# Attention over windows followed by a gated FFN: the third transposition of the probabilities moved into the dense tile, exponentials behind its copy, mixing and norms dealt to other slots

## The chip, the cores and the metric

The kernel runs on one core of a Trainium2 chip. The metric is the device time of one execution in microseconds; lower is better. All data is fp32.

## The reference

The input x is 4 x 2048 x 512. Cut to what matters, with `ln` the layer norm without weights:

```python
def attention(x):                       # x: (4, 2048, 512), 16 heads of 32, windows of 128
    q, k, v = split(x @ w_qkv, 3)
    k_ctx, v_ctx = windows n-1, n, n+1  # three blocks of 128 keys; outside the sequence masked
    attn = softmax((q * 32**-0.5) @ k_ctx.T)
    return attn @ v_ctx

def ffn(x):                             # H=512, F=2048, E=8 experts
    h = relu(x @ gate_w1.T + gate_b1)
    g = mean over the sequence of (h @ gate_w2.T + gate_b2)      # (batch, 8)
    mW1 = W1 + sum_e g[e] * TW1[e];  mb1 = b1 + g @ Tb1
    mW2 = W2 + sum_e g[e] * TW2[e];  mb2 = b2 + g @ Tb2
    return gelu(x @ mW1.T + mb1) @ mW2.T + mb2

x = x + ln(attention(ln(x)))
x = x + ln(ffn(ln(x)))
```

The expert weights are mixed once per batch element, after its gate is known.

## The kernel before

Every instruction's order is written out by hand; the engines work their queues in that order and wait for each other by semaphores. There are two stages: attention, with the gate and part of the mixing, and the FFN, which holds the rest of the mixing.

**Attention** runs over 256 slots, numbered i. A window W of 128 queries takes four slots, g = 0 to 3, of four heads each (i = 4W + g). In the loop of lines 550 to 577 slot i does this:

1. `first[i]`: loads.
2. `scores(i + 1)`: TensorE writes the scores of the next slot's four heads into two PSUM tiles `sc` of two heads each (L404), and VectorE takes the negated row maxima `nm` (L413). The pool `ps_s` has two buffers of such tiles: one slot's worth.
3. `turn(i, 0)` and `turn(i, 1)`: TensorE transposes the probabilities `pr` of key blocks 0 and 1 (L441), ScalarE copies the result to `prT` (L443). The pool `ps_t` has two buffers.
4. `exponentials(i + 1)`: four ScalarE activations read `sc` and `nm`, write `pr` and sum the rows into `den` (L426; each is followed by an accumulator read).
5. `dense[i]`, if there is one: one output tile of 128 x 512 of the projections to q, k or v (`project`, L353) or of the gate (`gate_matmuls`, L163), four matmuls in the program and eight in the trace, into the single buffer `pm`.
6. `turn(i, 2)`, if the window has three key blocks (the first and last window of a sequence have two).
7. The evacuation of the dense tile: q, v and the gate on ScalarE, k on VectorE (L359).
8. `aux[i]`, `values(i)` and the rest of `aux[i]`. `values` multiplies prT with v, key block by key block (L458). `aux` holds the transposition of the previous window's output with its scaling and statistics (g = 0, L223 to L236), that of the second norm (g = 3, L252 to L258), and `place_tile`, which transposes a tile of the next block of x after its norm (L339, L340).
9. `rest[i]`: the residual sum and its statistics (g = 1), the second norm (g = 2), and the first norm of a coming block: `norm_stats` and `norm_tile`, by VectorE with two small GpSimd operations.
10. From slot 84 on, one or two steps of `blend`, the mixer of lines 102 to 159.

A **block K** is four windows (512 rows). Its slots begin at s0 = 4 (4K - 5): in s0 to s0 + 3 its four tiles are placed, in the 12 slots after that its q, k and v are projected. The gate of an earlier block has the dense tiles of slots s0 to s0 + 3.

A **step of mixing** is one `acc + g[e] * expert[e]` over 128 x 1024 (L144), or, after the eighth expert, four smaller VectorE sums over quarters of the tile (L152 to L155). Loads of experts are issued on SyncE three steps ahead into four buffers. All loads and stores go through SyncE's queue.

The **FFN** stage takes 16 blocks, seven products each instead of eight by a Strassen-like scheme, with the remaining steps of mixing between them. It is not touched by the change.

Of the kernel before, what the change touches and what calls it, by code (L numbers as in the profile page):

```python
# [9 lines left out]
F32 = mybir.dt.float32  # L10
# [6 lines left out]
P = 128  # L17
NB, L, D = 4, 2048, 512
# [3 lines left out]
KC = D // P  # L22
TB = 512
# [11 lines left out]
def sandwich(ctx: ExitStack, tc: tile.TileContext, x, w_qkv, gw1, gb1, gw2, gb2, w1, b1, w2, b2, tw1, tb1, tw2, tb2, out):  # L35
# [49 lines left out]
    def stats(src, tag):  # L85

        st = small.tile([P, 6], F32, tag="st", name=f"st_{tag}")
        nc.vector.bn_stats(st, src)
        mv = small.tile([P, 2], F32, tag="mv", name=f"mv_{tag}")
        nc.vector.bn_aggr(mv, st)  # L90
        ve = small.tile([P, 1], F32, tag="ve", name=f"ve_{tag}")
        nc.gpsimd.tensor_scalar(ve, mv[:, 1:2], EPS, None, ALU.add)  # L92
        rs = small.tile([P, 1], F32, tag="rs", name=f"rs_{tag}")
        nc.gpsimd.tensor_tensor(rs, ve, mhalf, ALU.pow)
        return mv, rs

    def normalize(dst, src, sm):
        mv, rs = sm
        nc.vector.tensor_scalar(dst, src, mv[:, 0:1], rs, ALU.subtract, ALU.mult)
# [58 lines left out]
        for f in late:  # L158
            f()

    def gate_matmuls(pm, xT, oc):
        for kc in range(KC):
            nc.tensor.matmul(pm, lhsT=gw1_sb[:, kc, ts(oc, P)], rhs=xT[:, kc, :], start=(kc == 0), stop=(kc == KC - 1))  # L163

    def gate_sum(pm, K, oc, hsum, spare):
        hr = spare(f"hr_{K}_{oc}")
        k = K % NBLK
        nc.scalar.activation(hr, pm, AF.Relu, bias=gb1_sb[:, oc : oc + 1], accum_out=hsum[:, oc, k : k + 1])
# [120 lines left out]
    with ExitStack() as actx:  # L289
        qkvp = actx.enter_context(tc.tile_pool(name="qkvp", bufs=2))  # L290
        work = actx.enter_context(tc.tile_pool(name="work", bufs=2))
# [3 lines left out]
        ps_m = actx.enter_context(tc.tile_pool(name="ps_m", bufs=1, space=PSUM))  # L295

        def load_tile(K, t, tag, bufs):
            b, k = divmod(K, NBLK)
            xt = qkvp.tile([P, D], F32, tag=tag, bufs=bufs, name=f"{tag}_{K}_{t}")
            nc.sync.dma_start(xt, x[b, k * TB + t * P : k * TB + (t + 1) * P])  # L300
            return xt

        x_of, xs_of, xn_of, xnT_of, q_of, k_of, v_of, gT_of = {}, {}, {}, {}, {}, {}, {}, {}
# [21 lines left out]
        def norm_stats(K, t):  # L325
            xs_of[K, t] = stats(x_of[K, t], f"a{K}_{t}")

        def norm_tile(K, t):
            xn = work.tile([P, D], F32, tag="xn", name=f"xn_{K}_{t}")
            normalize(xn, x_of.pop((K, t)), xs_of.pop((K, t)))  # L330
            xn_of[K, t] = xn

        def place_tile(K, t, evac):
            if t == 0:
                xnT_of[K] = qkvp.tile([P, KC, TB], F32, tag="xnT", bufs=2, name=f"xnT_{K}")
            pt = ps_t.tile([P, KC, P], F32, tag="pt", name=f"pt_a{K}_{t}")
            xn = xn_of.pop((K, t))
            for kc in range(KC):
                nc.tensor.transpose(pt[:, kc, :], xn[:, ts(kc, P)], ident)  # L339
            evac(xnT_of[K][:, :, ts(t, P)], pt)  # L340

        def project(K, i, m, pm):

            if m == 0:
                d, name = (q_of, k_of, v_of)[i], "qkv"[i]
                d[K] = qkvp.tile([P, KC, TB], F32, tag=name, name=f"{name}_{K}")
            xnT = xnT_of[K]
            for kc in range(KC):
                if i < 2:
                    l, r = wqkv[i][:, kc, ts(m, P)], xnT[:, kc, :]  # L350
                else:
                    l, r = xnT[:, kc, ts(m, P)], wqkv[2][:, kc, :]
                nc.tensor.matmul(pm, lhsT=l, rhs=r, start=(kc == 0), stop=(kc == KC - 1))  # L353

        def projected(K, i, m, pm):
            if i == 0:
                nc.scalar.mul(q_of[K][:, m, :], pm, QSCALE)
            elif i == 1:
                nc.vector.tensor_copy(k_of[K][:, m, :], pm)  # L359
            else:  # L360
                nc.scalar.copy(v_of[K][:, m, :], pm)  # L361

        def span_of(W_):
            b, w = divmod(W_, NW)
            lo, hi = max(w - 1, 0), min(w + 1, NW - 1)
            return b * NW + lo, hi - lo + 1
# [51 lines left out]
        def exponentials(i):  # L418
            W_, g = divmod(i, KC)
            nk = span_of(W_)[1]  # L420
            st = win[W_]
            scs = st.pop(("sc", g))
            for r in range(4):
                h = g * 4 + r
                pr = work.tile([P, 3 * W], F32, tag="pr", bufs=8, name=f"pr_{i}_{r}")
                nc.scalar.activation(  # L426
                    pr[:, : nk * W],
                    scs[r // 2][:, r % 2, : nk * W],
                    AF.Exp,
                    bias=st["nm"][:, h : h + 1],  # L430
                    accum_out=st["den"][:, h : h + 1],
                )
                st["pr"][h] = pr

        def turn(i, j):

            W_, g = divmod(i, KC)
            st = win[W_]
            pt = ps_t.tile([P, 4, W], F32, tag="pt", name=f"ptp_{i}_{j}")
            for r in range(4):  # L440
                nc.tensor.transpose(pt[:, r, :], st["pr"][g * 4 + r][:, ts(j, W)], ident)  # L441
            prT = work.tile([P, 4, W], F32, tag="prT", bufs=4, name=f"prT_{i}_{j}")
            nc.scalar.copy(prT, pt)  # L443
            st["prT"][g, j] = prT
# [25 lines left out]
        dense = {i: None for i in slots}  # L470
        aux = {i: [] for i in slots}
        rest = {i: [] for i in slots}
        first = {i: [] for i in slots}
        for K in range(1, NBK):
            s0 = 4 * (4 * K - 5)
            if K > 1:
                for t in range(WB):
                    first[s0 + t - 6].append(lambda K=K, t=t: x_of.__setitem__((K, t), load_tile(K, t, "x", 4)))
                    rest[s0 + t - 3].append(lambda K=K, t=t: norm_stats(K, t))
                    rest[s0 + t - 2].append(lambda K=K, t=t: norm_tile(K, t))  # L480
                    aux[s0 + t].append(lambda K=K, t=t: place_tile(K, t, nc.vector.tensor_copy))
            for n, i in enumerate((0, 1, 2)):
                for m in range(KC):
                    dense[s0 + 4 + 4 * n + m] = (
                        lambda pm, K=K, i=i, m=m: project(K, i, m, pm),
                        lambda pm, K=K, i=i, m=m: projected(K, i, m, pm),
                    )

# [6 lines left out]
        def load_gate(K):  # L495
            gT_of[K] = qkvp.tile([P, KC, TB], F32, tag="xnT", bufs=2, name=f"gT_{K}")
            nc.sync.dma_start(gT_of[K], xT_d[K])

        gate_at = {K: 4 * (4 * (K + 3) - 5) for K in range(11)} | {11: 204, 12: 220, 13: 236, 14: 248}
        for K, s0 in gate_at.items():  # L500
            first[s0 - 2].append(lambda K=K: load_gate(K))
            for oc in range(KC):
                dense[s0 + oc] = (
                    lambda pm, K=K, oc=oc: gate_matmuls(pm, gT_of[K], oc),
                    lambda pm, K=K, oc=oc: gate_sum(pm, K, oc, hsum_of[K // NBLK], spare),
                )
            if K % NBLK == NBLK - 1:
                b = K // NBLK
                for j, f in enumerate(gate_end(b, hsum_of[b], spare, spare_bank)):
                    rest[s0 + KC + j].append(f)  # L510
# [19 lines left out]
        for t in range(WB):  # L530
            norm_tile(0, t)
            place_tile(0, t, nc.scalar.copy)
# [17 lines left out]
        for i in range(NS):  # L550
            W_, g = divmod(i, KC)
            nk = span_of(W_)[1]
            for f in first[i]:
                f()
            if i + 1 < NS:
                scores(i + 1)
            turn(i, 0)
            turn(i, 1)
            if i + 1 < NS:
                exponentials(i + 1)  # L560
            if dense[i]:
                pm = ps_m.tile([P, TB], F32, tag="pm", name=f"pm_{i}")
                dense[i][0](pm)
            if nk == 3:
                turn(i, 2)
            if dense[i]:
                dense[i][1](pm)
            for f in aux[i][:1]:
                f()
            values(i)  # L570
            for f in aux[i][1:]:
                f()
            for f in rest[i]:
                f()
            if i >= 84:
                for _ in range(1 if i % 3 == 2 else 2):
                    next(blend)


# [338 lines left out]
```

## Time and profile before

| | us |
|---|---|
| median of 3 runs | 3506.17 |
| lowest and highest | 3504.3, 3508.7 |
| profiled execution, its own time | 3506.56 |
| its span in the profile | 3504.8 |
| TensorE busy in the span | 3381.1 |
| VectorE busy | 2034.2 |
| ScalarE busy | 1476.4 |
| GpSimd busy | 734.2 |

A row of the timeline gives the start in us, the time from the start of the first to the end of the last instruction of a group, the engine, the line, the operation, output and inputs, how many, and in brackets how long the engine had been idle and what ended it. PE is TensorE, PEld its weight load, DVE VectorE, ACT ScalarE, POOL GpSimd, SPq the queue of DMA issues. A row of waits reads: who waited for whom, us in total, times, longest. A row of windows reads: the stretch and its length, the busy time and number of instructions of PE, PEld, DVE, ACT and POOL, the share of TensorE's clock that was granted, the DMA engines' share and GB/s.

### The profile page before, as it was taken

The page shows a single profiled execution, that of the slowest core. Times are in us where ns is not written, and L with a number is a line of the kernel's source. Part 1 is how long each engine was busy: PE and PEld are TensorE (multiplying, and loading weights), DVE is VectorE, ACT ScalarE, POOL GpSimd, SP SyncE. Part 2 cuts the span into 40 slices and gives each one's busy share as a digit, 9 for nine tenths or more (in the row PEclk, how much of TensorE's full clock was granted, in tenths as well). Part 3 has the DMA queues.
Part 4 walks back from the last instruction along what each step waited for, and adds up shares of the span by engine and source line. Part 5 has one row for each costly group of instructions (what it writes and reads, how often), then busy time and mean ns, then how long its engine had stood idle before and what let it go on. Part 6 is the DMA issues. An engine that isn't in the chain of part 4 may idle for free.

```text
span 3504.8 us, 55562 instructions
## 1 busy us (share of the span) xinstructions
PE 3381.1 (96%) x21712; PEld 2427.0 (69%) x21712; DVE 2034.2 (58%) x2868; ACT 1476.4 (42%) x3882; POOL 734.2 (21%) x776
## 2 busy tenths in 40 slices
PE   8999999999999999999988999999999999999998
PEld 4555555555555555555555888888888888888887
DVE  2545455677776777776776367666675774222222
ACT  2666666566565666665665222211112222221121
POOL 0100111122211221221111232223322332122222
PEclk9999999999999999999999999999999999999999
DMA  2111111355564555564567588998889885533332
GB/s 80 40 53 40 40 58 52 130 190 188 196 215 147 188 193 182 187 201 162 177 208 250 198 288 294 349 341 310 294 306 358 297 304 186 183 121 121 120 117 75
DMA packets 315192, 651.76 MB, mean 186 GB/s; under 512 B 22953, under 2 KB 88617, under 8 KB 294450
## 3 DMA queue, kind: packets, MB, share of 16 engines
q1 hardware_dynamic: 314930, 648.22, 53.4%
q8 instruction: 170, 2.79, 0.3%
q14 instruction: 92, 0.75, 0.1%
HBM read 538.03 MB, written 110.10 MB: 185 GB/s over the span
## 4 chain that ended last, share of the span: by engine, by line
PE 80%; DVE 9%; ACT 5%; DMA 3%; issue 2%; SPq 0%; ACTq 0%; DVEq 0%
PE pm L353 15%; PE px L600 11%; PE px L693 9%; PE ptp L441 8%; PE pz L693 6%; PE pz L600 5%; PE sc L404 5%; PE pm L163 5%; PE po L458 4%; DVE acc L144 3%; PE py L693 3%; ACT pr L426 3%; PE py L600 3%; PE py2b L693 3%; DMA exps<-in_tw 2%; ACT prT L443 2%
## 5 line engine op out<-in xcount | busy, mean ns | idle before, releaser
L144 DVE SCALAR_TENSOR_TENSOR acc<-exps,g,acc 128x1024 f32<-128x1024 f32 x512 | 690.5, 1349 | 210.0 <-DMA exps<-in_tw 205.4
L443 ACT COPY prT<-ptp 128x512 f32<-128x512 f32 x736 | 408.5, 589 | 544.8 <-PE ptp L441 544.4
L426 ACT ACTIVATE pr<-sc,nm 128x384 f32<-128x384 f32 (+1 forms) x1024 | 569.0, 576 | 130.5 <-DVE nm L413 130.2
L413 DVE TENSOR_REDUCE nm<-sc 128x2 f32<-128x768 f32 (+1 forms) x512 | 448.0, 916 | 255.7 <-PE sc L404 238.0
L441 PEld LDWEIGHTS ptp<-ident,pr 128*128 128x128 f32 x2944 | 342.3, 145 | 225.2 <-issue 209.0
L353 PE MATMUL pm<-xnT,wqkv 128*128 128x512 f32 x1024 | 465.5, 598 | 3.6 <-DVE k L359 1.6
L441 PE MATMUL ptp<-ident,pr 128*128 128x128 f32 x2944 | 429.5, 284 | 2.3 <-ACT prT L443 2.3
L600 PE MATMUL px<-tT,w 128*128 128x256 f32 x1536 | 359.1, 382 | 9.0 <-DVE cpv L658 9.0
L633 ACT COPY cpa<-px 128x512 f32<-128x512 f32 x64 | 37.2, 581 | 766.4 <-PE px L600 766.4
L600 PEld LDWEIGHTS px<-tT,w 128*128 128x128 f32 x1536 | 293.2, 191 | 51.5 <-DVE cpv L658 11.2
L353 PEld LDWEIGHTS pm<-xnT,wqkv 128*128 128x128 f32 x1024 | 187.0, 193 | 195.5 <-issue 188.1
L458 PE MATMUL po<-prT,v 128*32 128x128 f32 x5888 | 239.7, 281 | 79.8 <-ACT prT L443 79.6
L92 POOL TENSOR_SCALAR ve_b<-mv_b 128x1 f32<-128x1 f32 x64 | 43.6, 682 | 1174.3 <-DVE mv_b L90 1114.8
L404 PE MATMUL sc<-k,q 32*128 32x384 f32 (+2 forms) x2816 | 252.9, 437 | 5.1 <-ACT pr L426 3.8
L458 PEld LDWEIGHTS po<-prT,v 128*32 128x32 f32 x5888 | 138.8, 109 | 159.7 <-ACT prT L443 110.9
L353 PE MATMUL pm<-wqkv,xnT 128*128 128x512 f32 x512 | 230.5, 593 | 0.5 <-ACT v L361 0.5
L693 PE MATMUL px<-w2s,u 128*128 128x256 f32 x1024 | 229.7, 380 | 0.7 <-ACT last L257 0.7
L426 ACT ACTIVATION_READ_ACCUMULATOR pr<-sc,nm 128x1 f32 x1024 | 219.8, 215 | 0.0
L163 PE MATMUL pm<-gT,gw_sb 128*128 128x512 f32 x480 | 218.6, 598 | 0.0
L693 PEld LDWEIGHTS px<-w2s,u 128*128 128x128 f32 x1024 | 195.2, 191 | 27.7 <-ACT last L257 0.9
L670 POOL TENSOR_TENSOR t<-u 128x512 f32<-128x512 f32 x64 | 87.4, 1366 | 461.0 <-ACT u L612 448.9
L404 PEld LDWEIGHTS sc<-k,q 32*128 32x128 f32 x2816 | 122.1, 190 | 61.0 <-issue 39.3
(127 smaller groups left out, 4483.7 us busy)
## 6 DMA issues: line engine op xcount, KB each, us to landing
exps<-in_tw SPq DMA_DIRECT2D x512, 512.0 KB, 5.8
w2s<-m2d SPq DMA_DIRECT2D x112, 1024.0 KB, 5.6
acc<-in_w SPq DMA_DIRECT2D x64, 512.0 KB, 5.9
x<-in_x SPq DMA_DIRECT2D x64, 256.0 KB, 3.9
m1d<-acc SPq DMA_DIRECT2D x64, 256.0 KB, 6.0
m2d<-acc SPq DMA_DIRECT2D x64, 256.0 KB, 6.7
w<-m1d SPq DMA_DIRECT2D x16, 1024.0 KB, 9.4
fxT<-xTd SPq DMA_DIRECT2D x16, 1024.0 KB, 8.3
```

The costliest lines, as they stand in the source:

```text
L144: nc.vector.scalar_tensor_tensor(acc, ets.pop(n), g_all[b][:, e : e + 1], acc, ALU.mult, ALU.add)
L163: nc.tensor.matmul(pm, lhsT=gw1_sb[:, kc, ts(oc, P)], rhs=xT[:, kc, :], start=(kc == 0), stop=(kc == KC - 1))
L353: nc.tensor.matmul(pm, lhsT=l, rhs=r, start=(kc == 0), stop=(kc == KC - 1))
L404: nc.tensor.matmul(scs[r // 2][:, r % 2, col : col + nj * W], lhsT=q[rows, g, ts(W_ % WB, W)], rhs=k_of[kb][rows, g, j0 * W : (j0 + nj) * ...
L413: nc.vector.tensor_reduce(st["nm"][:, h : h + 2], scs[u][:, :, : nk * W], AX.X, ALU.max, negate=True)
L426: nc.scalar.activation(pr[:, : nk * W], scs[r // 2][:, r % 2, : nk * W], AF.Exp, bias=st["nm"][:, h : h + 1], accum_out=st["den"][:, h : h ...
L441: nc.tensor.transpose(pt[:, r, :], st["pr"][g * 4 + r][:, ts(j, W)], ident)
L443: nc.scalar.copy(prT, pt)
L458: nc.tensor.matmul(st["po"][r * E : (r + 1) * E, g, :], lhsT=v_of[kb][:, jj, h * E : (h + 1) * E], rhs=prT[:, r, :], start=(j == 0), stop= ...
L600: nc.tensor.matmul(bank[:, f, :], lhsT=factor[:, f, kc * P : (kc + 1) * P], rhs=right[:, kc, :], start=(start and f == 0 and kc == 0), sto ...
L670: nc.gpsimd.tensor_tensor(t1s[c], b12, S["u"][:, :, :Q], ALU.subtract)
L693: nc.tensor.matmul(bank[:, t, :], lhsT=right(c - c % 2)[:, c % 2, ts(t, P)], rhs=w[:, c, :], start=(start and c == t == 0), stop=True, ski ...
```

## The change

In the slot, the dense tile is split after two of its four matmuls. `turn(i, 2)` is put between the halves, and `exponentials(i + 1)` behind `turn(i, 2)`, so that on ScalarE the copy of the third transposition comes ahead of the exponentials. `project` and `gate_matmuls` get the range of matmuls to do.

The norm of a coming block's tile is written over its x tile, not into a tile of its own. For blocks 3 and up, tile t has its statistics in slot s0 - 14 + 4t and its norm in the slot after it, one tile per window; its load is issued two slots ahead of the statistics, at the end of a slot. For block 2 the statistics and the norm keep their slots, and the load moves by one.

From slot 84 on the four slots of a window take 1, 1, 2 and 3 steps of mixing, every third window 1, 1, 2 and 2, where each slot took 2, 2 and 1 in turn before.

```diff
         def norm_tile(K, t):
-            xn = work.tile([P, D], F32, tag="xn", name=f"xn_{K}_{t}")
-            normalize(xn, x_of.pop((K, t)), xs_of.pop((K, t)))
-            xn_of[K, t] = xn
+            xn = xn_of[K, t] = x_of.pop((K, t))
+            normalize(xn, xn, xs_of.pop((K, t)))
...
                 for t in range(WB):
-                    first[s0 + t - 6].append(lambda K=K, t=t: x_of.__setitem__((K, t), load_tile(K, t, "x", 4)))
-                    rest[s0 + t - 3].append(lambda K=K, t=t: norm_stats(K, t))
-                    rest[s0 + t - 2].append(lambda K=K, t=t: norm_tile(K, t))
+
+                    i = s0 - 14 + 4 * t if K > 2 else s0 + t - 3
+                    rest[i - 2].append(lambda K=K, t=t: x_of.__setitem__((K, t), load_tile(K, t, "x", 4)))
+                    rest[i].append(lambda K=K, t=t: norm_stats(K, t))
+                    rest[i + 1].append(lambda K=K, t=t: norm_tile(K, t))
                     aux[s0 + t].append(lambda K=K, t=t: place_tile(K, t, nc.vector.tensor_copy))
...
             turn(i, 0)
             turn(i, 1)
+            if dense[i]:
+                pm = ps_m.tile([P, TB], F32, tag="pm", name=f"pm_{i}")
+                dense[i][0](pm, range(KC // 2))
+            if nk == 3:
+                turn(i, 2)
             if i + 1 < NS:
                 exponentials(i + 1)
             if dense[i]:
-                pm = ps_m.tile([P, TB], F32, tag="pm", name=f"pm_{i}")
-                dense[i][0](pm)
-            if nk == 3:
-                turn(i, 2)
-            if dense[i]:
+                dense[i][0](pm, range(KC // 2, KC))
                 dense[i][1](pm)
...
             if i >= 84:
-                for _ in range(1 if i % 3 == 2 else 2):
+                for _ in range((1, 1, 2, 2 if W_ % 3 == 2 else 3)[g]):
                     next(blend)
```

More of the change, by code (lines that the diff above doesn't have):

```diff
@@ L159, in mixer, with gate_matmuls @@
             f()
-    def gate_matmuls(pm, xT, oc):
-        for kc in range(KC):
+    def gate_matmuls(pm, xT, oc, kcs=range(KC)):
+        for kc in kcs:
             nc.tensor.matmul(pm, lhsT=gw1_sb[:, kc, ts(oc, P)], rhs=xT[:, kc, :], start=(kc == 0), stop=(kc == KC - 1))
@@ L340, in place_tile, with project @@
             evac(xnT_of[K][:, :, ts(t, P)], pt)
-        def project(K, i, m, pm):
-            if m == 0:
+        def project(K, i, m, pm, kcs=range(KC)):
+            if m == 0 and kcs[0] == 0:
                 d, name = (q_of, k_of, v_of)[i], "qkv"[i]
@@ L347, in project @@
             xnT = xnT_of[K]
-            for kc in range(KC):
+            for kc in kcs:
                 if i < 2:
@@ L484, in sandwich @@
                     dense[s0 + 4 + 4 * n + m] = (
-                        lambda pm, K=K, i=i, m=m: project(K, i, m, pm),
+                        lambda pm, kcs, K=K, i=i, m=m: project(K, i, m, pm, kcs),
                         lambda pm, K=K, i=i, m=m: projected(K, i, m, pm),
@@ L503, in sandwich @@
                 dense[s0 + oc] = (
-                    lambda pm, K=K, oc=oc: gate_matmuls(pm, gT_of[K], oc),
+                    lambda pm, kcs, K=K, oc=oc: gate_matmuls(pm, gT_of[K], oc, kcs),
                     lambda pm, K=K, oc=oc: gate_sum(pm, K, oc, hsum_of[K // NBLK], spare),
```

## The prediction

> **What bounds the kernel now.** I read the page first, for the bound; then the waits, for what TensorE waits for; then the timeline slot by slot, since a share over the span mixes two stages. The attention stage, which alone is changed, runs from the start to about 1905 us.
>
> ```profile
> span 3504.8 us, 55562 instructions
> PE 3381.1 (96%) x21712; PEld 2427.0 (69%) x21712; DVE 2034.2 (58%) x2868; ACT 1476.4 (42%) x3882; POOL 734.2 (21%) x776
> ```
> ```profile
> ACT prT L443 <- PE ptp L441: 544.4, 432, 4.1
> ...
> ACT pr L426 <- DVE nm L413: 130.2, 92, 4.1
> ...
> PE po L458 <- ACT prT L443: 79.6, 108, 3.3
> ```
>
> TensorE is the bound, and its 124 us without work (3504.8 - 3381.1) are mostly one wait: values() on the copy of the transposed probabilities. Why that copy is late shows in a timeline. An undisturbed slot that also transposes an output:
>
> ```profile
> 798.23 0.93 PE L404 MATMUL sc<-k,q 32*128 32x384 f32 x8
> ...
> 799.09 1.09 PE L441 MATMUL ptp<-ident,pr 128*128 128x128 f32 x8
> ...
> 800.01 3.60 PE L353 MATMUL pm<-wqkv,xnT 128*128 128x512 f32 x8
> ...
> 800.79 0.60 ACT L426 ACTIVATE pr<-sc,nm 128x384 f32<-128x384 f32 x1
> ...
> 802.93 0.23 ACT L426 ACTIVATION_READ_ACCUMULATOR pr<-sc,nm 128x1 f32 x1
> ...
> 803.45 0.60 PE L441 MATMUL ptp<-ident,pr 128*128 128x128 f32 x4
> ...
> 804.14 0.59 ACT L443 COPY prT<-ptp 128x512 f32<-128x512 f32 x1 [0.98 <-PE ptp L441]
> ...
> 805.21 0.93 PE L404 MATMUL sc<-k,q 32*128 32x384 f32 x8
> ```
>
> From scores to scores 6.98 us, all of it TensorE's. Without an output transposition the slot takes 6.91: values() then stands 0.16 us before its third block, because the last copy begins only 0.69 us after the third transposition, and TensorE loses as much again in draining. In a slot where VectorE is late it looks like this:
>
> ```profile
> 836.54 2.57 DVE L144 SCALAR_TENSOR_TENSOR acc<-exps,g,acc 128x1024 f32<-128x1024 f32 x2
> ...
> 839.03 1.82 DVE L413 TENSOR_REDUCE nm<-sc 128x2 f32<-128x768 f32 x2
> ...
> 840.02 0.58 ACT L426 ACTIVATE pr<-sc,nm 128x384 f32<-128x384 f32 x1 [3.68 <-DVE nm L413]
> ...
> 842.26 0.60 ACT L443 COPY prT<-ptp 128x512 f32<-128x512 f32 x1
> ...
> 842.91 0.65 PE L458 MATMUL po<-prT,v 128*32 128x128 f32 x8 [2.41 <-ACT prT L443]
> ```
>
> VectorE still mixes two experts while the row maxima are due; the exponentials wait for the maxima, the copy behind them on ScalarE waits too, TensorE waits for the copy. I compared each slot from 84 on (where mixing begins) with undisturbed slots of its kind. Lost by lateness: 29 us in the 28 three-block slots that place a new block (their norms and statistics lie just before and in them), 19 us in the other three-block slots, 6 us in two-block ones: 54 us. The slots around the three gate ends lose 29 us (some of it their own matmuls), those without a dense tile 41 us.
>
> **What is removed.** (1) values() no longer needs a copy that stands behind the exponentials. (2) Statistics and norms of a block, four tiles in five adjoining slots, become one tile per window, in slots 2 and 3. (3) Mixing becomes 1, 1, 2, 3 (every third window 2) instead of 2, 2, 1: 20 steps in 12 slots both ways, so nothing moves to the FFN stage. VectorE's load of a window, from the rows: maxima 4 x 1.82, output scaling and its statistics 1.8 in slot 0, residual and statistics 2.1 in slot 1, second norm 0.53 in slot 2, seven steps of about 1.35: 21 us in 27, or 22.5 with a tile's 0.87 of statistics and 0.53 of norm. It fits; only the order was bad. New worst cases: a k-slot (evacuation 0.69, ready only when the dense tile ends) with three mixing steps lets the next maxima start at about 3.2 us after the first transpositions, against 2.8 wanted below: 0.3 to 0.5 us, in 11 windows; the placing slots 2 and 3 are like it. I leave 10 us of the 54. Gain 44 (bounds 20 and 54).
>
> **A rule of the skill here.** After each of the five 2.41 us waits in placing slots the granted clock is halved, and the next slot is 1.2 to 2.8 us too long, 9 us together (inside the 29):
>
> ```profile
> 833.60:842.60 9.00, 6.89 (x57) 4.34 (x56) 8.69 (x14) 3.66 (x11) 3.73 (x4) 1.00 0.22 61
> 842.70:846.10 3.40, 3.19 (x29) 2.48 (x30) 3.30 (x5) 0.83 (x3) 1.90 (x2) 0.50 0.58 172
> ```
>
> The Trainium skill ("TensorE: Matmul & The Clock Gate", Part 1) says that TensorE falls to half rate after an idle window of about 3.4 us. By it a 2.41 us wait costs only itself, the half-rate stretches have another cause, and the gain is 35 (in the sum below 30 for 39). By the trace, five of five follow such a wait at once and, in slots with a dense tile, none follows a wait up to 1.5 us: they go with it. I take the trace, 44.
>
> **What is added.** The exponentials of i+1 now stand behind the third copy, and the scores of i+2 overwrite their banks: two tiles per slot, two buffers. The rows of a two-block slot show the hand-over:
>
> ```profile
> 959.94 0.21 ACT L426 ACTIVATION_READ_ACCUMULATOR pr<-sc,nm 128x1 f32 x1
> ...
> 960.20 0.70 PE L404 MATMUL sc<-k,q 32*128 32x256 f32 x4 [0.21 <-ACT pr L426]
> ...
> 960.83 1.09 PE L441 MATMUL ptp<-ident,pr 128*128 128x128 f32 x8
> ```
>
> The second pair of scores starts 0.05 after the last accumulator read, and, coming after the first pair, takes as long alone as all four together (0.63 here; 0.86 for three blocks, 798.23 to 799.09). That closes a ring through two engines: scores pair 0.86, transpositions 0.92 (799.09 to 800.01), half the dense tile 1.72 (four matmuls of 0.43), third transposition to its copy 0.69 (803.45 to 804.14), copy to first exponential 0.48, four exponentials with their reads 2.37 (800.79 to 803.16), hand-over 0.05: 7.09, say 7.08 us. TensorE's own work is 6.54 without and 6.98 with an output transposition, so the ring becomes the bound by a little. Of 256 slots 212 have three blocks and a dense tile (28 have two blocks and keep their order, 16 have no dense tile). 40 of the 212 place a tile: TensorE has 7.0 to 7.6 us of work there, no loss. The other 172, half of each kind: 86 x (7.08 - 6.91) + 86 x (7.08 - 6.98) = 23 us lost. Bounds of the ring: 6.54 where the wait is hidden altogether (gain 30), and 7.4 if each of the six links is some 0.05 longer; I take 7.08 since every link is a row.
>
> Behind the later exponentials on ScalarE stand the evacuations of q, v or the gate (0.60 to 0.90), of the second norm's transposition and of the output (0.53, 0.58). They end about 1.7 us after the last exponential, just when the next copy can begin (0.86 + 0.75): nothing, as long as the ring is over 7.0; at 6.7 some 0.3 us in each last slot of a window, 15 us. The wait of the pending x1 and xT stores on SyncE grows by about 2 us; mixing loads behind them are three steps ahead, 6 us or more, so nothing; without that lead three steps in a row would meet loads of 5.8 us. The x loads now go into a buffer that the placing transpositions free, and the first one of a block stands on SyncE until slot 0's placement; two slots of 7 us remain before its statistics. VectorE's normalising in place costs the same 0.53, and saves the prologue's 1.1 us waits for transpositions: 1 us at most. Splitting the dense tile costs nothing by the rows (transposition to dense and back without a gap); at most 0.09 a slot, 20 us, within the ring's bound.
>
> **Gate ends and slots without a dense tile.** The three gate ends: values() waits of 1.5 to 3.3 us, then a halved clock; with values() free and fewer steps in slots 1 and 2, I take 12 of 29 (5 to 20). Without a dense tile the ring is shorter by 1.7 and a TensorE gap takes its place, about 5.6 for 5.85: with smoother VectorE work 5 us in 16 slots (0 to 12).
>
> **Sum.** 44 + 12 + 5 + 1 - 23 = 39 us off the profiled execution's 3506.6 (span 3504.8 and 1.8 around it), which stands 0.4 above the median: 3467. FFN, TensorE-bound with its mixing steps unchanged, starts that much earlier.
>
> **Rivals.** A: no new wait. If a score pair needs no pause, the slots fall to TensorE's 6.54 and the small waits are saved (30) instead of 23 lost: 92 us, 3414. For it: VectorE and ScalarE have spare time; against: the two rows of 959.94. B: the deal doesn't do what it says. Three steps in slot 3 and k's evacuation keep the lateness: no 44, net +5, 3511. For it: maxima waited in just such slots; against: the sum of 22.5 in 27 us and the 1.1 us of additional room before exponentials. C, slower: the score wait takes the place of the copy's wait. Place: second score pair on the last exponential, in all 172 slots; price: 172 us for each us of ring. From 7.3 it eats the 39 us; at 7.45 the time is 3530. For it: it stands in every slot, where lateness stood in some 60; against: each link is measured.
>
> **How the numbers follow.** Main case 0.60, own range 3443 to 3490 (ring 7.0 to 7.2, lateness 35 to 54). A 0.13, B 0.12, C 0.15. About 0.2% (7 us) is what a measurement of this kernel can tell from no change. Faster: main, A and a third of B, 0.77; same 0.08 from B and C; slower 0.15. The range 3414 to 3508 takes in main, most of A and a part of B.
>
> **What would show it.** After: "po <- prT" nearly gone from the waits, "sc <- pr" new with some 60 to 100 us; undisturbed slots of 7.0 to 7.2 us, in the first 600 us too, so that slots 4 to 83 get slower; no 2.41 us waits and fewer half-clock stretches; placing windows shorter by 4 us each. Undisturbed slots of 6.6 prove A, 7.4 prove C; maxima still ending the exponentials' wait prove B.

## The result and the profile after

The changed kernel takes 3475.4 us in the median (3468.1 to 3477.9) against 3506.2: a ratio of 0.9908, interval 0.9891 to 0.9925. The prediction was 3467 in a range of 3414 to 3508, and 3443 to 3490 for its main case alone. The profiled execution has a span of 3476.1 us, 28.7 less than before.

The page's first lines of the kernel after:

```profile
span 3476.1 us, 56070 instructions
PE 3411.5 (98%) x21712; PEld 2453.0 (71%) x21712; DVE 2037.5 (59%) x2868; ACT 1472.0 (42%) x3882; POOL 690.4 (20%) x776
```

The same 21712 matmuls are "busy" for 30 us more (3411.5 against 3381.1) in a span that is 29 us shorter. TensorE's idle time fell from 124 to 65 us, and only half of that came off the span. In these rows a matmul that begins late beside its neighbours counts as busy (score groups of 1.65 and 1.89 us below). The new loss has to be looked for inside the busy time.

Some waits of the kernel after:

```profile
ACT pr L425 <- DVE nm L412: 19.9, 16, 2.1
...
PE sc L403 <- ACT pr L425: 11.0, 27, 1.5
PEld pb L207 <- ACT q L356: 7.9, 3, 3.3
PE pb L207 <- ACT q L356: 7.1, 3, 3.1
...
PE pg L187 <- ACT q L356: 2.9, 3, 1.0
PE pz L602 <- DMA w<-m1d: 2.8, 1, 2.8
...
PE po L457 <- ACT prT L442: 0.6, 3, 0.3
```

values() waits 0.6 us for the copies instead of 79.6, and the exponentials wait 19.9 us for late maxima instead of 130.2. New are waits for the evacuation of q (the products `pg` and `pb` of the gate ends). The 11.0 us in which scores wait for exponentials lie in slots without a dense tile or beside them, and in two-block slots; in the slots with three blocks and a dense tile the exponentials cost TensorE time that has no wait by name. An undisturbed slot with an output transposition, timeline of the kernel after:

```profile
1022.38 0.22 ACT L425 ACTIVATION_READ_ACCUMULATOR pr<-sc,nm 128x1 f32 x1
...
1022.54 1.03 PE L403 MATMUL sc<-k,q 32*128 32x384 f32 x8
...
1023.50 1.09 PE L440 MATMUL ptp<-ident,pr 128*128 128x128 f32 x8
...
1024.43 1.88 PE L352 MATMUL pm<-wqkv,xnT 128*128 128x512 f32 x4
1026.15 0.60 PE L440 MATMUL ptp<-ident,pr 128*128 128x128 f32 x4
...
1026.84 0.59 ACT L442 COPY prT<-ptp 128x512 f32<-128x512 f32 x1 [1.52 <-PE ptp L440]
1027.32 0.59 ACT L425 ACTIVATE pr<-sc,nm 128x384 f32<-128x384 f32 x1
...
1029.46 0.22 ACT L425 ACTIVATION_READ_ACCUMULATOR pr<-sc,nm 128x1 f32 x1
...
1030.59 1.09 PE L440 MATMUL ptp<-ident,pr 128*128 128x128 f32 x8
```

The ring that the prediction added up is there link by link: from the last accumulator read's end (1022.60) to the transpositions 0.90, to the dense tile 0.93, half of it 1.72, to the copy 0.69, to the first exponential 0.48, to the end of the last read 2.36. From transposition to transposition 7.09 us; the forecast had 7.08. The second score pair's pause is hardly visible as a wait: the group of eight takes 1.03 where it took 0.93, because the first pair still runs when the second begins.

Slot by slot, worked out from the traces, in us against before. A slot is taken from its first score product to that of the next slot. The start with slot 0, the last four slots and the 12 placing slots ahead of mixing, together -1 to -5, are left out of the rows. The last three columns are experiments told below:

| slots, number | after | order alone | deal alone | one of four |
|---|---|---|---|---|
| placing, mixing runs, 28 | -25.4 | -11.9 | -20.7 | -27.2 |
| other three-block, mixing runs, 110 | -3.6 | -0.8 | -11.4 | -33.7 |
| other three-block, before mixing, 53 | +7.3 | +7.6 | 0.0 | -8.2 |
| two-block, 27 | -3.4 | +0.1 | -3.4 | -3.4 |
| at the gate ends, three each, 9 | -2.2 | -0.9 | -6.6 | -5.2 |
| without a dense tile, 12 | -7.1 | -8.7 | +1.4 | -8.8 |
| from start to the FFN's first product | -35.2 | -17.5 | -45.3 | -91.4 |
| FFN | +6.5 | -4.0 | +7.7 | +7.0 |
| whole span | -28.7 | -21.5 | -37.5 | -84.4 |

### The profile page after: what moved, and what is told of

It reads as the page before. It is cut to its first block, busy times and chain, and to the rows that moved or that the text cites. A ratio compares the mean times of both kernels' runs of the same rounds, so it can differ in the third digit from the quotient of the medians.

```text
span 3476.1 us, 56070 instructions
## 1 busy us (share of the span) xinstructions
PE 3411.5 (98%) x21712; PEld 2453.0 (71%) x21712; DVE 2037.5 (59%) x2868; ACT 1472.0 (42%) x3882; POOL 690.4 (20%) x776
## 4 chain that ended last, share of the span: by engine, by line
PE 92%; DMA 3%; DVE 2%; ACT 2%; issue 1%; SPq 0%; ACTq 0%; DVEq 0%
PE pm L352 19%; PE px L602 11%; PE ptp L440 10%; PE px L695 9%; PE sc L403 8%; PE pz L695 6%; PE pm L163 6%; PE pz L602 6%; PE po L457 5%; PE py L695 3%; PE py2b L695 3%; PE py L602 3%; DMA exps<-in_tw 2%; ACT pr L425 1%; PE pto L223 1%; PE ptx L252 1%
## 5 line engine op out<-in xcount | busy, mean ns | idle before, releaser
L425 ACT ACTIVATE pr<-sc,nm 128x384 f32<-128x384 f32 (+1 forms) x1024 | 569.0, 575 | 20.1 <-DVE nm L412 19.9
L352 PE MATMUL pm<-xnT,wqkv 128*128 128x512 f32 x1024 | 485.9, 602 | 3.6 <-DVE k L358 1.6
L403 PE MATMUL sc<-k,q 32*128 32x384 f32 (+2 forms) x2816 | 306.8, 425 | 11.0 <-ACT pr L425 11.0
L352 PEld LDWEIGHTS pm<-xnT,wqkv 128*128 128x128 f32 x1024 | 180.0, 194 | 146.6 <-issue 139.3
L352 PE MATMUL pm<-wqkv,xnT 128*128 128x512 f32 x512 | 240.4, 593 | 0.5 <-ACT v L360 0.5
L403 PEld LDWEIGHTS sc<-k,q 32*128 32x128 f32 x2816 | 159.7, 184 | 86.0 <-issue 47.2
L457 PEld LDWEIGHTS po<-prT,v 128*32 128x32 f32 x5888 | 145.9, 110 | 103.1 <-issue 93.9
L457 PE MATMUL po<-prT,v 128*32 128x128 f32 x5888 | 216.9, 279 | 0.8 <-ACT prT L442 0.6
```

The lines of the kernel that those rows point to most:

```text
L403: nc.tensor.matmul(scs[r // 2][:, r % 2, col : col + nj * W], lhsT=q[rows, g, ts(W_ % WB, W)], rhs=k_of[kb][rows, g, j0 * W : (j0 + nj) * ...
L425: nc.scalar.activation(pr[:, : nk * W], scs[r // 2][:, r % 2, : nk * W], AF.Exp, bias=st["nm"][:, h : h + 1], accum_out=st["den"][:, h : h ...
L457: nc.tensor.matmul(st["po"][r * E : (r + 1) * E, g, :], lhsT=v_of[kb][:, jj, h * E : (h + 1) * E], rhs=prT[:, r, :], start=(j == 0), stop= ...
```

## The experiments

The theory was that the change is two changes that pay separately: the deal of VectorE's work removes the lateness, and the order costs a ring in every slot. Four kernels were set against it.

**The order alone.** From after, mixing, statistics and norms put back (the norm into a tile of its own too, not shown):

```diff
...
-                    i = s0 - 14 + 4 * t if K > 2 else s0 + t - 3
...
+                    first[s0 + t - 6].append(lambda K=K, t=t: x_of.__setitem__((K, t), load_tile(K, t, "x", 4)))
+                    rest[s0 + t - 3].append(lambda K=K, t=t: norm_stats(K, t))
+                    rest[s0 + t - 2].append(lambda K=K, t=t: norm_tile(K, t))
...
-                for _ in range((1, 1, 2, 2 if W_ % 3 == 2 else 3)[g]):
+                for _ in range(1 if i % 3 == 2 else 2):
```

> The kernel before with the new order of a slot alone; mixing and norms as before. Theory (two effects that pay separately: the ring of second score pair, transpositions, half the dense tile, third copy and exponentials costs 0.14 us in each of some 170 undisturbed slots, 23 us; the new deal of VectorE's work is what takes the 54 us of lateness away): undisturbed slots of 7.09 us on the mean, the 2.41 us waits shrink by the 1.1 us of added room for the maxima, lateness falls by some 30 us; the whole is 3480 to 3505. Rival (the order makes the gain, the deal little): 3480 or less, as after. Second rival (the order alone only costs): 3520 or more.

Measured: 3492.9 us, ratio 0.9953 (0.9937 to 0.9968). This is inside the theory's span; both rivals fall. In the slots before mixing the ring costs 7.6 us, as in after. While mixing runs, the other three-block slots come out even: the added room for late maxima pays the ring's cost. What stays is about half of the lateness in the placing slots, which win 11.9 us where they win 25.4 in after.

**The deal alone.** From after, the slot's order put back:

```diff
+            if i + 1 < NS:
+                exponentials(i + 1)
             if dense[i]:
                 pm = ps_m.tile([P, TB], F32, tag="pm", name=f"pm_{i}")
-                dense[i][0](pm, range(KC // 2))
+                dense[i][0](pm, range(KC))
             if nk == 3:
                 turn(i, 2)
-            if i + 1 < NS:
-                exponentials(i + 1)
             if dense[i]:
-                dense[i][0](pm, range(KC // 2, KC))
                 dense[i][1](pm)
```

> The kernel after with the order of a slot of before: exponentials ahead of the dense tile, third transposition behind it. Theory of separate effects: no ring, so undisturbed slots of 6.91 and 6.98 us; the maxima come early enough by the deal alone except in slots with k's evacuation and three mixing steps (some 10 us left); the FFN begins with the same 4 us loss as in the kernel after. The whole is 3455 to 3470, faster than the kernel after by 5 to 20 us. Rival (the later exponentials are needed to cover VectorE): the 0.7 to 1.3 us waits of values() stay in most windows, 3480 to 3500.

Measured: 3467.1 us, 0.9881 (0.9864 to 0.9897): in the theory's span and 8 us faster than the kernel after in the median. The intervals of the two ratios just overlap; in the profiles, the FFN's first product comes 10.1 us earlier than in after. The slots before mixing are those of before to the hundredth. Its wait of values():

```profile
PE po L457 <- ACT prT L442: 51.5, 124, 3.3
```

Of these 51.5 us, 13 are the 0.16 us of 83 slots, 21 lie in the twelve slots without a dense tile (0.9 to 2.8 each), and 8.6 at the gate ends (2.1, 3.3 and 3.3). The rest is some 0.2 to 0.7 each, for the most part in and after the placing slots. So the order, as it was placed, cost time on top of the deal.

The two parts don't add: in the profiles they win 21.5 and 37.5 us alone and 28.7 together. Both take lateness away, so the theory of two separate effects holds for the ring and not for the lateness. In the slots without a dense tile the gain is the order's (8.7 alone, against a loss of 1.4 by the deal alone).

**The place of the third transposition.** If the ring is the cost, it has a length to set: the matmuls of the dense tile that stand ahead of the third transposition, 0.86 us each in the program's count. From after:

```diff
-                dense[i][0](pm, range(KC // 2))
+                dense[i][0](pm, range(1))
...
-                dense[i][0](pm, range(KC // 2, KC))
+                dense[i][0](pm, range(1, KC))
```

> The kernel after with the third transposition behind one of the four matmuls of a dense tile, not two. Ring theory: the ring is 0.86 us shorter, 6.23 us, below TensorE's own 6.54 and 6.98; undisturbed slots fall to 6.54 and 6.98, second score pairs wait hardly any more, 172 slots gain 57 us less some lateness (maxima are due 0.86 us sooner): 3420 to 3440. Rival (the 7.09 us slots come from splitting a dense tile or from the drain around the third transposition, wherever it lies): within 5 us of the kernel after.

Measured: 3420.6 us, 0.9746 (0.9732 to 0.9761). The timeline of its slot without an output transposition:

```profile
757.65 0.93 PE L403 MATMUL sc<-k,q 32*128 32x384 f32 x8
758.51 1.09 PE L440 MATMUL ptp<-ident,pr 128*128 128x128 f32 x8
...
760.30 0.60 PE L440 MATMUL ptp<-ident,pr 128*128 128x128 f32 x4
...
763.62 0.22 ACT L425 ACTIVATION_READ_ACCUMULATOR pr<-sc,nm 128x1 f32 x1
764.20 0.93 PE L403 MATMUL sc<-k,q 32*128 32x384 f32 x8
```

The last read ends (763.84) before the scores begin, and the slot takes 6.55 us: TensorE's own work. The time is near the one that rival A had forecast, but it is reached by a shorter ring, not by score pairs that need no pause.

With `range(3)` and `range(3, KC)`, three of four matmuls ahead:

> The kernel after with the third transposition behind three of the four matmuls. Ring theory: the ring is 0.86 us longer, 7.95 us, in all 212 slots with three blocks and a dense tile, the placing ones too: 172 x 0.86 + 40 x 0.6 = 172 us, 3635 to 3655. Rival (the split itself, not its place): within 5 us of the kernel after.

Measured: 3644.9 us, 1.0388 (1.0373 to 1.0404), in the span of the ring theory. One slot in its timeline:

```profile
848.52 1.89 PE L403 MATMUL sc<-k,q 32*128 32x384 f32 x8
...
850.34 1.09 PE L440 MATMUL ptp<-ident,pr 128*128 128x128 f32 x8
...
853.84 0.60 PE L440 MATMUL ptp<-ident,pr 128*128 128x128 f32 x4
```

The next transpositions begin at 858.28: 7.94 us from transposition to transposition, 0.85 more than after. The split tile as such shows no cost (6.55 us with one matmul ahead, where TensorE's own work was put at 6.54); its place sets the time.

With `range(0)` and `range(KC)`, the transposition ahead of the whole tile (`project` then makes its output tile by another test, not shown):

> The kernel after with the third transposition straight behind the second, ahead of the whole dense tile. Ring theory: the ring is 5.4 us and no bound; but the third transposition needs the bank of the first, whose copy is ready 0.3 us too late, and TensorE loses 0.5 us as in slots without a dense tile: 212 slots of some 7.04 and 7.48 us, 106 us over the version with one matmul ahead: 3515 to 3530, slower than before. Rival (the shorter the ring the faster): 3420 or less.

Measured: 3518.8 us, 1.0033 (1.0026 to 1.0041), slower than before. Timeline of one slot:

```profile
797.20 1.09 PE L440 MATMUL ptp<-ident,pr 128*128 128x128 f32 x8
797.95 1.08 ACT L442 COPY prT<-ptp 128x512 f32<-128x512 f32 x2 [3.26 <-PE ptp L440]
798.59 0.66 PE L440 MATMUL ptp<-ident,pr 128*128 128x128 f32 x4 [0.29 <-ACT prT L442]
799.08 3.60 PE L352 MATMUL pm<-xnT,wqkv 128*128 128x512 f32 x8
```

No ring, but the third transposition waits 0.29 us for the copy that empties the first one's bank, and the dense tile starts 1.88 us after the first transposition, half a us more than twelve transpositions take at the rate of the first eight (1.5 x 0.92 us). The slots take 7.06 us without and 7.50 with an output transposition, 0.5 more than with one matmul ahead, which covers this copy.

**Which part of the deal matters.** On the one-of-four version, with mixing as before (the last lines of the first diff) and with norms as before (its middle lines, the normalising still in place):

> The version with the third transposition behind one of four matmuls, with the mixing steps of before (2, 2, 1 in turn), norms as after. Theory (with no ring there is less slack for late maxima, and two steps in slots 0 and 1 make them late as before): 10 to 25 us over that version, 3430 to 3446, waits of scores on exponentials where values() waited before. Rival (the norms alone were the burden on VectorE): within 5 us of it, 3416 to 3426.

> The version with the third transposition behind one of four matmuls, with the statistics and norms of a block in the five slots of before, mixing 1, 1, 2, 3 as after. Theory (norms burden only the seven placing windows in which mixing runs): those 28 slots lose 10 to 15 us again, the other slots nothing: 3430 to 3437. Rival (mixing alone was the burden): within 4 us, 3416 to 3425.

Measured: 3440.9 us with the old mixing (0.9811, 0.9791 to 0.9832), 20 more than with the new. Up to the FFN it is 28 us longer in the profiles, and the FFN 10 us shorter (the part on the last window tells why in part). With the old norms it takes 3422.2 (0.9754, 0.9733 to 0.9775), not to be told from the one-of-four version. Timeline with the old mixing:

```profile
760.50 0.95 DVE L412 TENSOR_REDUCE nm<-sc 128x2 f32<-128x768 f32 x1
...
760.62 0.58 ACT L425 ACTIVATE pr<-sc,nm 128x384 f32<-128x384 f32 x1 [0.94 <-DVE nm L412]
...
762.30 1.65 PE L403 MATMUL sc<-k,q 32*128 32x384 f32 x8
```

Late maxima now show as a score group of 1.65 us, again without a wait of a matmul by name. For the mixing the theory held, for the norms its rival did: their 28 slots lost 3.1 us (24.2 won instead of 27.2), where 10 to 15 were expected. So the burden was the deal of the mixing. In the three-block slots with a dense tile, 19.4 us of its cost lie in slots 2 and 3 of the windows and none in slots 0 and 1. That fits too many steps in slots 0 and 1, but no run tests single slots.

**The gate ends.** Timeline of the kernel after at the second gate end:

```profile
1103.19 0.58 ACT L425 ACTIVATE pr<-sc,nm 128x384 f32<-128x384 f32 x1 [2.00 <-DVE nm L412]
...
1105.43 0.61 ACT L356 ACTIVATE q<-pm 128x512 f32<-128x512 f32 x1
1106.09 2.07 PE L207 MATMUL pb<-tb_sb,gcb 8*128 8x512 f32 x2 [3.07 <-ACT q L356]
```

The product `pb` needs the dense tile's bank; q leaves it only behind the exponentials, which here wait for maxima besides. The experiment gives these products a bank of the transpositions:

```diff
         def spare_bank(name):
-            return ps_m.tile([P, TB], F32, tag="pm", name=name)
+            return ps_t.tile([P, TB], F32, tag="pt", name=name)
```

> The kernel after with the small products of the gate ends in a bank of the transpositions, not in the dense tile's. The trace of after has TensorE waiting 1.0 and 3.1 us for ScalarE's evacuation of q ahead of these products at each gate end: the dense tile's bank is freed behind the later exponentials. Theory (this new wait is why the gate ends gained only 2 us where 12 were forecast): the two waits go, three gate ends win 2 to 4 us each, 6 to 12 us together: 3463 to 3470. Rival (the gate ends are held by VectorE's long list there, the bank is only the last in line): the waits turn into waits on VectorE, under 3 us in all: 3472 to 3476.

Measured: 3456.2 us, 0.9855 (0.9841 to 0.9870), 19 less than after. The same products of the second gate end:

```profile
1092.91 0.86 PE L457 MATMUL po<-prT,v 128*32 128x128 f32 x24
1093.70 1.12 PE L207 MATMUL pb<-tb_sb,gcb 8*128 8x512 f32 x2
1093.94 0.58 ACT L425 ACTIVATE pr<-sc,nm 128x384 f32<-128x384 f32 x1 [2.00 <-DVE nm L412]
```

The wait for the maxima is still there (2.00), now beside the products. The three slots of the second gate end take 25.8 us instead of 32.0, those of the first 23.2 instead of 30.2, of the third 26.1 instead of 32.1: 19.3 together. The theory was right and its size too small. The waits by name were 1.9, 4.0 and 4.0 us, and it had not counted what follows them. In after the granted clock is 0.50 for 10.2 us at each gate end (at the second from 1105.3 to 1115.6, and the two `pb` products take 2.1 us there instead of 1.1). With the other bank it is 0.50 for 0, 3.4 and 3.4 us. If the work of those stretches runs at half speed, an estimate from these figures, their 24 us fewer are worth up to 12.

**The last window.** SyncE's issues where the FFN begins, kernel after:

```profile
1875.14 0.58 SPq L116 DMA_DIRECT2D acc<-in_w  x1
1875.82 1.49 SPq L119 DMA_DIRECT2D exps<-in_tw  x3
1877.35 5.32 SPq L284 DMA_DIRECT2D w<-m1d  x7
```

Four loads of 512 KB go out ahead of the FFN's weights, and TensorE waits 2.8 us for those. The experiment on after:

```diff
-                for _ in range((1, 1, 2, 2 if W_ % 3 == 2 else 3)[g]):
+                for _ in range((2, 2, 2, 1)[g] if W_ == NWA - 1 else (1, 1, 2, 2 if W_ % 3 == 2 else 3)[g]):
```

> The kernel after with the seven mixing steps of the last window dealt 2, 2, 2, 1 instead of 1, 1, 2, 3. The trace of after has the FFN's first weights issued behind the loads of three late steps: TensorE waits 2.8 us for them (1.2 before), its clock is halved after that, and the first FFN block takes 3.7 us more than before. Theory (the deal of the last window is the cause): the wait is 1.2 us or less again and the first block wins 3 to 4 us: 3470 to 3474. Rival (chance of the DMA queues): no change of that wait, 3475.

Measured: 3462.6 us, 0.9880 (0.9865 to 0.9895), 13 less than after and 7 less than forecast. One such load goes ahead, the wait is gone, and the FFN's first block wins 4.6 us, a little over the forecast. The first block takes 121.2 to 123.5 us in the seven profiled kernels that deal 1, 1, 2, 3 to the end, and 116.5 to 117.5 in the five that don't (before, order alone, old mixing, this one and the last one below), so the deal of the last window is its cause. The rest of the gain isn't explained by it: 4.5 us lie ahead of the FFN, where the two programs are the same nearly throughout, and 4.4 in later blocks. From the second block to the end the FFN takes 1473.8 to 1480.0 us with 1, 1, 2, 3 in the last window and 1474.3 to 1478.3 without, so that deal doesn't set the later blocks. What does stays open.

**All three together**, one of four matmuls ahead, the other bank and the last window:

> The version with the third transposition behind one of four matmuls, with the gate ends' products in the transpositions' bank and the last window's steps dealt 2, 2, 2, 1. Theory: the three changes hit different stages and add up; the gate ends lose less here already, since the exponentials come 0.86 us sooner, so 8 to 15 us for them and 0 to 4 for the last window: 3402 to 3412. Rival (they cover the same time): within 5 us of 3421.

Measured: 3400.0 us, 0.9691 (0.9673 to 0.9709): the fastest of all, 75 us under after and 2 under the theory's span. Against one of four alone the ratio falls by 0.0055, 19 us. In the profiles the gate ends win 16.5 and the FFN 6.5 of it, the first block 5.5, so the changes add up in different places, as the theory had it. The sizes are over its upper ends of 15 and 4.

## Why the prediction was right

Its main case came about: lateness went, a ring came, and the difference is the gain. The sum was 39 us, and the medians show 31 (the profiles 29). Two terms, the gate ends and the FFN, were too large by 10 and 6.5 us; lateness and the slots without a dense tile gave 4 and 2 more than forecast, so some errors offset each other. The range of 3414 to 3508 takes in rival A's time and no change as well. The rows of the ring and the moves of the transposition say more for the mechanism than the time does.

- Lateness: 44 us forecast. Measured 47.6: 25.4 in the placing slots, 3.4 in two-block ones, and 18.8 in the other 110 slots (3.6 won there, and 15.2 of ring paid there, if it costs the 0.138 us per slot that it costs before mixing). By the same slots the deal alone wins 35.5, so some 12 us of the 47.6 come from the later exponentials.
- The ring: 7.08 us forecast, 7.09 measured; 23 us of cost forecast, 22.5 measured (163 slots at 0.138). Its mechanism, and that it outweighs the copy wait that it removes, is shown by the deal alone and by the places of the transposition, one and three matmuls ahead. It could be forecast so closely because every link stood as a row in the trace of before.
- The clock: no half-rate stretch is left in the placing slots. At the place of the first of the five, kernel after:

```profile
843.00:846.50 3.50, 3.50 (x54) 2.92 (x53) 2.78 (x6) 2.51 (x9) 0.00 (x0) 1.00 0.07 20
```

  Where the 2.41 us waits went, the half-rate stretches went with them. That fits the trace's reading and not an idle window of about 3.4 us, as the Trainium skill ("TensorE: Matmul & The Clock Gate", Part 1) has it, so the 9 us belong to the gain. It is no rule by the length of a wait: at the first gate end of after a stretch begins (637.7) behind a wait of 0.97 us, and with the other bank two begin at gate ends (1097.6 and 1551.5) where TensorE has no gap over 0.9 us. What starts these isn't shown. The stretches that remain in the attention stage of after lie at its two ends, in slots without a dense tile, and at the gate ends.
- Gate ends: the term that was mis-sized. 12 us forecast, 2.2 measured. The prediction listed the evacuations of q, v and the gate as standing behind the later exponentials, and priced them at nothing by asking only when ScalarE's next copy can begin. It did not ask who waits for the bank that they free: the gate ends' products do, 1.0 to 3.1 us. With a bank of the transpositions these slots give another 19.3 us.
- FFN: "starts that much earlier", with nothing lost, was wrong by 6.5 us, of which 3.7 lie in the first block and go with the last window's deal; the cause of the others, in blocks 4 and 8, is open. The prediction had counted mixing steps (20 in 12 slots both ways, 287 in all) and not the loads in SyncE's queue ahead of the FFN's weights.
- Slots without a dense tile: 5 forecast, 7.1 measured, by the order and not by VectorE's smoother work.
- Of the signs, "sc <- pr" at 60 to 100 us of wait was wrong: 11.0 on the matmuls and 36.8 on the weight loads. The 11.0 aren't even the ring's: with one matmul ahead, without a ring, they are 11.3. In the ring's slots the first score pair covers the second one's pause, and the loss stands in TensorE's busy time.
- The 1 us for normalising in place was not tested alone.

Rival A was wrong: late score pairs cost what the ring says. Its time was nearly reached with one matmul ahead, by a shorter ring. Rival B fell with the 19.9 us of waits for maxima. Rival C's point, 7.3 us of ring, was not reached; three of four matmuls show what it would have cost.

## What to carry to other kernels

When an operation is moved behind another on a second engine, follow the chain until it comes back to the first engine, add its links from the rows, and compare the sum with that engine's own work per round: the bound is the larger one, and a move by one instruction (0.86 us here) can decide. For everything that then finishes later, ask for all users of the buffer that it frees, the rare ones too. Test the parts of a combined change apart: here one half of it alone earned 42 us (3506.2 x 0.0119), and the other half, on top of that, took 8 away. Put one matmul earlier it added 46 instead.

## What the runs showed that was not expected

- TensorE's busy time went up by 30 us for the same matmuls while the span fell by 29: four score products that use different rows run side by side in 0.86 us, and when the second two come late, both pairs together take 1.65 us (the run with the old mixing) or 1.89 (three of four matmuls ahead) and are counted as busy in one row.
- A third transposition straight after the first two costs 0.5 us per slot, of which 0.29 stand as a wait for the 0.59 us copy of the first one's bank; one matmul of 0.86 us in between makes it free.
- At a gate end, another bank for two small products gave 6 to 7 us where the waits by name were 1.9 to 4.0: the clock stood at half for 10.2 us there, and for 0 to 3.4 with the other bank.
